# An edge-gated graph layer on one core: from step 10 on the loads of h are issued by ScalarE's queue, GpSimd issues only gathers, and group 1's rows are made in other steps

## The chip, the cores and the metric

One core of a Trainium2 chip. The time is device microseconds of one execution; the median over the runs is told. The engines are TensorE (PE; PEld its weight loads), VectorE (DVE), ScalarE (ACT), GpSimd (POOL) and SyncE (SP). Transfers between the memories are issued by SP, ACT or POOL and carried by 16 transfer engines that all issuers share.

## The reference

B = 16 batches, N = 1024 nodes, D = 256 features, one dense adjacency `A` of 1024×1024 whose entries are mostly zero (a random symmetric pattern of density near 0.8% and the diagonal).

```python
pre_u  = einsum('bud,dk->buk', h, W1[:d])
pre_v  = einsum('bvd,dk->bvk', h, W1[d:])
hidden = relu(pre_u[:, :, None] + pre_v[:, None] + b1)
S      = sigmoid(einsum('buvk,ko->buvo', hidden, W2)[..., 0] + b2)
a      = einsum('buv,bud->bvd', S * A, h)
m      = einsum('uv,bud->bvd', A, h) * h
z      = beta1*h + beta2*(a @ Wa + ba) + beta3*(m @ Wm + bm)
```

The kernel evaluates `hidden` and `S` only where `A` is not zero.

## The kernel before

**Tiles and steps.** The 16 batches form four groups g of four. The 1024 nodes v form eight row blocks vt of 128. A block (g, vt) is worked in T = 10 steps, two windows of 64 nodes times five slots of 128 edges. The 32 blocks make 320 steps n; their order is group 0's vt 0 to 5, group 1's vt 0 to 5, then vt 6 and 7 of both, then groups 2 and 3 whole. For each group a table in device memory holds, per node u, the row of products h·W1[:d] (4×256 numbers) and the row of h (as many).

**One step.** `fetch(n)` is a gather issued by GpSimd: 128 rows of the table, 1 MB, into one of eight buffers `fetched`. `expand` (TensorE, tile `pc`) lays the receiving nodes' products beside the edges. `add` (VectorE) adds both; four VectorE operations make the scores; ScalarE takes the sigmoid (`gt`) and scales the edges' one-hot columns (`left`); `aggregate` (TensorE, tile `acc`) sums the edges into nodes. Buffers come free there, and `refill()` then issues the gather eight steps ahead. Another small gather, `fetch_val` (tile `val`), brings the edges' weights. After every second step ScalarE copies `acc` out (`ev`); at a window's end the sums are turned over (tile `LT`), and `block_end` multiplies them with `w_a` and `w_m` and stores the rows.

**The neighbour lists.** `lists(vt)` makes the edges of a row block: it loads 128 columns of the adjacency (`key`, 512 KB), picks the entries with VectorE, marks the edges' nodes (`mark`, rounded to bytes as `few`), and copies each mark to both halves of `whose` by four transfers of 40 KB. Lists 0 to 3 are made in the prologue, 4 to 7 are begun at steps 7, 14, 44 and 82.

**The tables.** `rows(k)` makes 128 rows of a table in two pieces. A piece is eight products of h with `w_u` on TensorE, a copy by ScalarE (tile `tab`) and a store by SyncE (L442); h itself goes from x into the table by `copy_h` on SyncE (L408). Group 0's rows are all made in the prologue, their stores (`table<-fetched`, L444) on SyncE. For the other groups `plan` names the two steps in which the pieces of a block are made, and `made_rows(n)` loads h for them (`load_hT`, L403, tiles `hT` and `wide`, 512 KB) as soon as a buffer is free and the first piece is at most 14 steps away (`AHEAD`). `again` names blocks whose h is loaded a second time for the block's own products.

**Order.** Each engine works its own instructions in the order in which the code issues them; a scheduler sets the semaphores between engines. The prologue is a written script: each letter of `script` issues a row piece (r), a block's products (h), the first eight gathers (f), one stage of a list (a digit), and so on. `after(step, f)` defers f to that step, `do(step)` calls it. SP and ACT together go round eight completion semaphores for their transfers, GpSimd round eight others; an issue waits until the transfer eight places earlier on its round has landed. In the orders below a row is an instruction's line, its kind, what it writes and reads, and the shape; `x4` counts like rows that follow one another.

Of the kernel before, what the change touches and what calls it, by code (L numbers as in the profile page):

```python
# [11 lines left out]
ALU = mybir.AluOpType  # L12
AX = mybir.AxisListType
P = 128
# [3 lines left out]
def kernel(  # L18
# [42 lines left out]
    nc = tc.nc  # L61
    B, N, D = x.shape
    NT = N // P
    DC = D // P
# [3 lines left out]
    W = 64  # L68
    NW = P // W
# [19 lines left out]
    def load_rows(src, n, name, engine=nc.scalar, at_=None):  # L89
        t = const.tile([P, n], FP, name=name) if at_ is None else at_  # L90
        engine.dma_start(t, bass.AP(tensor=src.tensor, offset=src.offset, ap=[[0, P], [1, n]]))
        return t

    def load_weights(src, name, engine=nc.scalar):
        t = const.tile([P, DC, D], FP, name=name)
        engine.dma_start(t, src.rearrange("(c p) k -> p c k", p=P))
        return t
# [3 lines left out]
    def fixed(shape, name, dt=FP):  # L101
        return const.tile(shape, dt, name=name)
# [74 lines left out]
    def spread(parts, v):  # L177
        nc.vector.tensor_copy(parts, v)
        nc.vector.tensor_tensor(parts[W:], v[W:], parts[W:].bitcast(FP), ALU.subtract)
        nc.vector.tensor_scalar(parts, parts.bitcast(FP), edge, None, ALU.mult)  # L180

    b1_p = fixed([P, D], "b1_p", FR)
    bias_p = fixed([P, D], "bias_p", FR)
# [5 lines left out]
    whose = const.tile([P, NT * NW, E], mybir.dt.uint8, name="whose")  # L189
# [31 lines left out]
    EARLY = 4  # L221
# [13 lines left out]

    def lists(vt):
        key = fetched[vt + 1][:, :N] if vt < EARLY else lst.tile([P, N], FP, name="key", bufs=1)
        (nc.sync if vt < EARLY else nc.gpsimd).dma_start(key, adjT[vt * P:(vt + 1) * P, :])
        yield "load"
        R = Rs[vt % EARLY]  # L240
        top = R[:, 4:]
# [64 lines left out]
        nc.scalar.activation(mark, mark, AF.Sign, bias=span[:, 0:1], scale=-1.0)  # L306
        nc.scalar.activation(mark, mark, AF.Relu)
        yield "step"
        if vt < EARLY:
            nc.scalar.copy(few, mark)  # L310
        else:
            nc.gpsimd.tensor_copy(few, mark)
        for w in range(NW):
            for h in range(2):
                nc.gpsimd.dma_start(whose[h * W:(h + 1) * W, vt * NW + w, :], few[w * W:(w + 1) * W])
        pe = aside(vt)
        for j in range(TW):
            nc.tensor.matmul(pe[:, j * NW * RC:(j + 1) * NW * RC], mark[:, j * P:(j + 1) * P],
# [54 lines left out]
    def after(step, f):  # L373
        due.setdefault(step, []).append(f)
# [8 lines left out]
    hTs = {}  # L383
# [16 lines left out]
    def load_hT(k, engine=nc.sync):  # L400
        g, nt = k
        hTs[k] = hT_free.pop(0)
        engine.dma_start(hTs[k].rearrange("p b c n -> p (b c) n"),  # L403
                         xT_rows[:, g * GB * DC:(g + 1) * GB * DC, nt * P:(nt + 1) * P])
# [95 lines left out]
    T = TW * NW  # L500
# [40 lines left out]
    for i in range(COPIES):  # L541
        copy_h(turn[i], nc.sync)

    script = ("r r 0 0", "r r 1 0 0", "r r 1", "r 0 0", "r r 1", "0 2 r 1", "0 0 r r", "1 2 r 1", "v r r 2", "r 1 3",
              "h 2 1 1", "h 2 2 3", "f 2 2 2 w h h h", "m 3 w 3 3 3")
    begun_rows = {}
    marks, pcs, accs, evs, hbs, LTs, lefts = {}, {}, {}, {}, {}, {}, {}

# [4 lines left out]
    def warm(times):  # L553
        acc = psa.tile([P, 2, D], FP, name="acc")
        for i in range(times):
            nc.tensor.matmul(acc, unit, b1_p.unsqueeze(1).to_broadcast([P, 2, D]), start=True, stop=True)

    m = 0
    piece = None
    parts = halves(0)  # L560
    for t, turns_ in enumerate(script):
        step = t - 100
        do(step)
        for c in turns_.split():
            if c == "r":
                k = turn[m % NT]
                if m < NT:
                    begun_rows[k] = rows(k, tabs[m])
                    next(begun_rows[k])
                go(begun_rows[k], step)  # L570
                if m > NT and m - NT + COPIES <= NT:
                    copy_h(turn[m - NT + COPIES - 1], nc.sync)
                m += 1
            elif c == "h":
                go(parts, step)
            elif c == "v":
                fetch_val(3)
                spread(b1_p, b1_b)
                next(parts)
            elif c == "f":  # L580
                for n in range(NF):
                    fetch(n)
                    if n > 2:
                        fetch_val(1)
                    if n in (3, 6):
                        load_hT(turn[NT + n // 6], nc.gpsimd)
                next(made[EARLY])
                w_a = load_weights(Wa, "w_a", nc.gpsimd)
                w_m = load_weights(Wm, "w_m", nc.gpsimd)
            elif c == "m":  # L590
                load_mark(0)
            elif c == "w":
                warm(6)
            else:
                next(made[int(c)], None)
    do(len(script) - 100)

    def scale_late():
        nc.vector.tensor_scalar(ba_b, ba_b, be2, None, ALU.mult)
        nc.vector.scalar_tensor_tensor(bias, bias, be3, ba_b, ALU.mult, ALU.add)  # L600
        spread(bias_p, bias)
        nc.vector.tensor_scalar(ba_c, ba_c, be2, None, ALU.mult)
        nc.vector.scalar_tensor_tensor(bias_c, bias_c, be3, ba_c, ALU.mult, ALU.add)
        nc.scalar.activation(w_a, w_a, AF.Copy, scale=be2)
        nc.scalar.activation(w_m, w_m, AF.Copy, scale=be3)
        hT_free.append(spare_)

# [190 lines left out]
    def plan(blocks, ns):  # L800

        for k, pieces in zip(blocks, ns):
            pending.append((pieces[0], k))
            at.update((n, k) for n in pieces)

    plan(turn[NT:], ((2, 4), (8, 9), (10, 15), (19, 20), (25, 29), (30, 35), (39, 40), (45, 47)))
    for g, first in ((2, 60), (3, 140)):
        plan([(g, vt) for vt in range(NT)], ((first + 9 + 10 * i, first + 14 + 10 * i) for i in range(NT)))
    pending.extend((order.index(k) * T - T + 1, k) for k in again)
# [2 lines left out]

    def made_rows(n):
        nonlocal piece, last
        while pending and (pending[0][1] in hTs or hT_free and pending[0][0] - AHEAD <= n):
            k = pending.pop(0)[1]
            if k not in hTs:
                load_hT(k, nc.gpsimd if n < T else nc.sync)
        if n in at:
            if at[n] != last:  # L820
                last = at[n]
                copy_h(last, nc.sync)
                piece = rows(last)
                next(piece)
            go(piece, n)
# [58 lines left out]
    for n in range(total - 3):  # L884
        k, s = divmod(n, T)
        if n < ROOM:
            gather_to(n - 1)
        pair_ends()
        if n % TW == (n < ROOM) and n // TW + 1 < total // TW:
            load_mark(n // TW + 1)  # L890
        expand(n + 2)
        if n >= ROOM:
            fill(n, False)
        products(n, k, s)
        if n >= ROOM and n % 2 == 0:
            gather_to(n)
        add(n + 1)
        gate(n)
        while behind:
            nc.scalar.copy(*behind.pop(0))  # L900
        do(n)
        if n == 1:
            bias = load_rows(bm, D, "bias", nc.sync, spare[:, 1])
            ba_b = load_rows(ba, D, "ba_b", nc.sync, spare[:, 2])
            bias_c, ba_c = fixed([P, DC], "bias_c"), fixed([P, DC], "ba_c")
            nc.sync.dma_start(bias_c, bm.rearrange("(c p) -> p c", p=P))
            nc.sync.dma_start(ba_c, ba.rearrange("(c p) -> p c", p=P))
            be1 = load_rows(beta1, 1, "be1", nc.sync)
            be2 = load_rows(beta2, 1, "be2", nc.sync)
            be3 = load_rows(beta3, 1, "be3", nc.sync)  # L910
            after(10, scale_late)
        if n == total - 6:
            hbs[BS - 1] = next(t for t in hT_free if t in flat).rearrange("p b c n -> p b (c n)")
            for v, m, f in tails:
                for h, o in tail_rows(x, v, m, f):
                    nc.sync.dma_start(h, o)
        for i in advance.get(n, ()):
            next(made[i], None)
        if n in start_list:
            running.append([made[start_list[n]], True, n])  # L920
            piece_of(running[-1], n)
        if n < ROOM:
            fill(n, False)
        if n == LISTS:
            assert not running and all(next(x, None) is None for x in made)
            lists_done()
            more = main.enter_context(tc.tile_pool(name="more", bufs=1))
            flat.extend(hT_places(more, MORE, NH))
            hT_free.extend(flat[-MORE:])
            minus.append(more.tile([P, P], FR, name="minus"))  # L930
            nc.vector.tensor_scalar(minus[0], ident, -1.0, None, ALU.mult)
        if n == 120:
            nc.vector.tensor_tensor(rest, rest, taken, ALU.subtract)
            nc.gpsimd.partition_all_reduce(longest, rest, P, bass_isa.ReduceOp.max)
            after(n + 12, count_rest)
# [152 lines left out]
```

## Time and profile before

| quantity | value |
|---|---|
| median of 3 runs | 1040.96 us (1038.32 to 1042.02) |
| profiled execution | 1031.14 us |
| its span | 1029.3 us |
| busy: PE, DVE, ACT, POOL | 958.9, 950.4, 886.5, 467.5 us |
| share of 16 transfer engines: GpSimd's gathers, SP's queue, ACT's queue | 76.1%, 20.3%, 0.2% |
| moved | 375.00 MB, 364 GB/s |
| addition of step 0, 7, 8, 12, 20, 50 starts | 58.49, 79.67, 90.00, 111.43, 138.84, 247.88 us |

The profile is of one execution, and its time is 1% below the median of the runs, so terms from the trace are set against its own time. The share of a queue is the time of its packets, as a share of the 16 engines' span. A later block of ten steps takes some 27.5 us. From the additions in the table one reads that the first twelve steps took 52.9 us, about 4.4 each, where later ones take 2.75.

### The profile page before, as it was taken

How to read it: one execution, taken by the hardware profiler on the slowest of the kernel's cores; microseconds unless marked ns; L12 is line 12 of the kernel's file. 1: busy time of each engine (PE TensorE's matmuls, PEld its weight loads, DVE VectorE, ACT ScalarE, POOL GpSimd, SP SyncE). 2: the span in 40 equal slices, each digit the busy share in tenths (PEclk: the TensorE clock that was granted, in tenths of full speed). 3: DMA queues.
4: the chain of work that ended last, by engine and by line, in shares of the span. 5: the costliest groups of instructions: out<-in, count | busy, mean ns of one | idle time of the engine just before them, and what ended most of it. 6: DMA issues, size and time to landing. Idle time of an engine off the chain costs nothing.

```text
span 1029.3 us, 21645 instructions
## 1 busy us (share of the span) xinstructions
PE 958.9 (93%) x6408; PEld 700.3 (68%) x6408; DVE 950.4 (92%) x3302; ACT 886.5 (86%) x2750; POOL 467.5 (45%) x487
## 2 busy tenths in 40 slices
PE   7886789999899999999999999999999999999996
PEld 5754566676567766767677777777777766777663
DVE  7585979988999999998999999999999999999994
ACT  3665777888888989989899999999999999999984
POOL 3367676746246433564333334333343344444430
PEclk9988899999999999999999999999999999999998
DMA  9898998999999999999999999999999999999992
GB/s 326 304 371 305 350 327 287 332 382 343 360 330 334 378 412 392 381 355 391 411 412 408 414 403 413 401 404 408 391 418 390 379 370 364 381 362 378 373 360 73
DMA packets 123199, 375.00 MB, mean 364 GB/s; under 512 B 17616, under 2 KB 76496, under 8 KB 86864
## 3 DMA queue, kind: packets, MB, share of 16 engines
q0 software_dynamic: 50976, 302.73, 76.1%
q1 hardware_dynamic: 71472, 70.27, 20.3%
q8 instruction: 53, 0.87, 0.3%
q10 hardware_dynamic: 624, 0.52, 0.2%
q14 instruction: 74, 0.61, 0.1%
HBM read 377.53 MB, written 50.33 MB: 416 GB/s over the span
## 4 chain that ended last, share of the span: by engine, by line
PE 45%; DVE 28%; issue 12%; ACT 7%; DMA 5%; POOL 2%; another core or an unknown queue 1%; POOLq 0%; DVEq 0%; SPq 0%; ACTq 0%
DVE fetched L653 15%; PE misc L414 13%; DVE fetched L646 11%; PE misc L740 9%; PE pc L616 8%; PE acc L669 8%; PE misc L691 4%; DMA fetched<-table,uidx 3%; ACT left L660 2%; POOL fetched L516 2%; DVE LT L708 1%; PE misc L724 1%; DMA val<-in_adjT_dram,vidx 1%; DMA wide<-in_xT_dram 1%; DVE low L477 1%
## 5 line engine op out<-in xcount | busy, mean ns | idle before, releaser
L516 POOL DMA_INDIRECT fetched<-table,uidx x320 | 342.7, 1071 | 464.6 <-PE acc L669 318.9
L653 DVE SCALAR_TENSOR_TENSOR fetched<-fetched,w_b 128x256 f32<-128x256 f32 x1280 | 476.7, 425 | 0.0
L646 DVE TENSOR_TENSOR fetched<-fetched,pc 128x1024 f32<-128x1024 f32 x320 | 389.8, 1218 | 43.0 <-DMA fetched<-table,uidx 13.8
L660 ACT ACTIVATE left<-left,gt 128x16 f32<-128x16 f32 x1280 | 285.7, 298 | 0.0
L616 PE MATMUL pc<-X,mark 128*128 128x512 f32 x640 | 227.5, 450 | 21.6 <-DVE fetched L646 17.3
L669 PE MATMUL acc<-fetched,left 128*32 128x256 f32 x2560 | 189.9, 388 | 13.0 <-ACT gt L656 4.5
L616 PEld LDWEIGHTS pc<-X,mark 128*128 128x128 f32 x640 | 105.9, 190 | 108.9 <-issue 55.0
L669 PEld LDWEIGHTS acc<-fetched,left 128*32 128x32 f32 x2560 | 74.4, 109 | 92.9 <-issue 30.0
L656 ACT ACTIVATE gt<-sc,b_b 128x4 f32<-128x4 f32 x320 | 96.7, 302 | 39.4 <-DVE fetched L653 31.6
L740 PE MATMUL misc<-w_a,LT 128*128 128x256 f32 x496 | 117.6, 380 | 1.6 <-issue 1.0
L740 PE MATMUL misc<-w_m,LT 128*128 128x256 f32 x496 | 117.3, 380 | 0.0
L653 DVE DVE_READ_ACCUMULATOR fetched<-fetched,w_b 128x1 f32 x1280 | 108.7, 85 | 0.0
L740 PEld LDWEIGHTS misc<-w_a,LT 128*128 128x128 f32 x496 | 93.8, 190 | 16.6 <-issue 1.4
L677 ACT COPY ev<-acc 128x512 f32<-128x512 f32 x160 | 92.2, 577 | 9.8 <-PE misc L414 5.2
L414 PE MATMUL misc<-w_u,wide 128*128 128x256 f32 x384 | 93.4, 392 | 7.2 <-DMA w_u<-in_W_dram 7.1
L624 ACT ACTIVATE left<-onehot,val 128x32 f32<-128x32 bf16 x320 | 99.9, 312 | 0.0
L356 POOL DMA_INDIRECT val<-in_adjT_dram,vidx x80 | 84.9, 1062 | 26.2 <-issue 21.0
L740 PEld LDWEIGHTS misc<-w_m,LT 128*128 128x128 f32 x496 | 89.7, 191 | 9.7
L691 PE MATMUL misc<-ident,ev 128*128 128x128 f32 x642 | 82.8, 274 | 7.1 <-ACT ev L677 3.0
L414 PE MATMUL misc<-w_v,wide 128*128 128x256 f32 x368 | 88.4, 384 | 0.0
L414 PEld LDWEIGHTS misc<-w_u,wide 128*128 128x128 f32 x384 | 74.7, 197 | 19.8 <-DMA w_u<-in_W_dram 7.1
L691 PEld LDWEIGHTS misc<-ident,ev 128*128 128x128 f32 x642 | 74.0, 141 | 17.1 <-ACT ev L677 4.1
(167 smaller groups left out, 1007.6 us busy)
## 6 DMA issues: line engine op xcount, KB each, us to landing
table<-in_x_dram SPq DMA_DIRECT2D x32, 512.0 KB
out_dram<-z SPq DMA_DIRECT2D x62, 256.0 KB
table<-tab SPq DMA_DIRECT2D x48, 256.0 KB
wide<-in_xT_dram SPq DMA_DIRECT2D x16, 512.0 KB
fetched<-table,uidx POOLq DMA_INDIRECT x320
wide<-in_xT_dram SPq DMA_DIRECT2D x4, 1024.0 KB
table<-fetched SPq DMA_DIRECT2D x8, 512.0 KB
hT<-in_xT_dram SPq DMA_DIRECT2D x8, 512.0 KB
```

The costliest lines, as they stand in the source:

```text
L414: nc.tensor.matmul(p[:, bb * D:(bb + 1) * D], hT[:, 2 * h + bb, i, :], wt[:, i, :], start=(i == 0 and not begun), stop=(i == DC - 1), skip ...
L516: nc.gpsimd.indirect_dma_start(out=fetched[at_slot[n]], out_offset=None, in_=table[g], in_offset=bass.IndirectOffsetOnAxis(ap=uidx[:, vt * ...
L616: nc.tensor.matmul(pcs[n][:, c], marks[n // TW][:, j * P:(j + 1) * P], cuts[k][w][:, c], start=True, stop=True)
L624: nc.scalar.activation(lefts[n][:, 1::GB, :], onehot[:, vt * NW + w, j, :].unsqueeze(1).to_broadcast([P, GB // 2, V]), AF.Copy, scale=val[ ...
L646: nc.vector.tensor_tensor(t, t, pcs.pop(n), ALU.add)
L653: nc.vector.scalar_tensor_tensor(t[:, b, :], t[:, b, :], 0.0, w2_b, ALU.max, ALU.mult, accum_out=sc[:, b:b + 1])
L656: nc.scalar.activation(gt, sc, AF.Sigmoid, bias=b2_b)
L660: nc.scalar.activation(lefts[n][:, 2 * b, :], lefts[n][:, 1 + b // 2 * GB, :], AF.Copy, scale=gt[:, b:b + 1])
L669: nc.tensor.matmul(accs[i][b * 2 * V:(b + 1) * 2 * V, r, :], left[:, 2 * b - b % 2:2 * b - b % 2 + 2].rearrange("p k v -> p (k v)"), f[:, ...
L677: nc.scalar.copy(evs[i], accs.pop(i))
L691: nc.tensor.matmul(pt[:, :, FROM[j]:FROM[j] + V], evs[i][:, r, c * P:(c + 1) * P], ident, is_transpose=True, start=(j == of[0]), stop=True ...
L740: nc.tensor.matmul(pz[:, bb * D:(bb + 1) * D], LT[:, 2 * h + bb, i if bb else 1 - i, c, :], wt[:, c, :], start=(i == 1 and bb == 0 and c = ...
```

## The change

Four parts. (A) GpSimd issues nothing but gathers: the `key` loads of lists 4 to 7, the loads of `w_a` and `w_m`, and all 32 transfers of marks into `whose` go from SyncE; lists 4 to 7 have `few` copied by ScalarE, as 0 to 3 have already. (B) In the prologue the loads of h for group 1's first two blocks move: (1,6) to a new letter k of the script, (1,7) to step 0, both on SyncE; `w_a`, `w_m` and the key of list 4 are loaded at step 0. The bias rows' loads are written in the prologue, and their scaling on VectorE (`scale_bias`, which also frees a buffer for h) is its last letter, s; the scaling of `w_a` and `w_m` stays at step 10. (C) Group 1's row pieces are made in other steps. (D) `made_rows` looks 6 steps ahead before step 10 and 14 after, and loads on SyncE before step 10 and on ScalarE's queue from then on.

```diff
 def lists(vt):
-    (nc.sync if vt < EARLY else nc.gpsimd).dma_start(key, ...)
+    nc.sync.dma_start(key, ...)
...
-    if vt < EARLY:
-        nc.scalar.copy(few, mark)
-    else:
-        nc.gpsimd.tensor_copy(few, mark)
+    nc.scalar.copy(few, mark)
...
-            nc.gpsimd.dma_start(whose[...], few[w * W:(w + 1) * W])
+            nc.sync.dma_start(whose[...], few[w * W:(w + 1) * W])
...
-    ..., "f 2 2 2 w h h h", "m 3 w 3 3 3")
+    ..., "f 2 2 2 k w h h h", "m 3 w 3 3 3 s")
...
+def scale_bias():           # the five VectorE lines of scale_late (seven operations)
+    ...
+    hT_free.append(spare_)
...
         fetch(n)
-        if n in (3, 6):
-            load_hT(turn[NT + n // 6], nc.gpsimd)
-    next(made[EARLY])
-    w_a = load_weights(Wa, "w_a", nc.gpsimd)
-    w_m = load_weights(Wm, "w_m", nc.gpsimd)
+    bias = load_rows(bm, D, "bias", nc.sync, spare[:, 1])
+    ...                      # ba_b, bias_c, ba_c, be1, be2, be3 as before
+elif c == "k":
+    load_hT(turn[NT])
+elif c == "s":
+    scale_bias()
...
-plan(turn[NT:], ((2, 4), (8, 9), (10, 15), (19, 20), (25, 29), (30, 35), (39, 40), (45, 47)))
+plan(turn[NT:], ((4, 6), (9, 11), (13, 18), (19, 21), (23, 28), (29, 31), (33, 38), (39, 41)))
...
-while pending and (... pending[0][0] - AHEAD <= n):
+while pending and (... pending[0][0] - (AHEAD if n >= T else 6) <= n):
-        load_hT(k, nc.gpsimd if n < T else nc.sync)
+        load_hT(k, nc.scalar if n >= T else nc.sync)
...
-if n == 1:
-    bias = load_rows(...)    # and the other seven
-    after(10, scale_late)
+if n == 0:
+    for i in advance[0]:
+        next(made[i], None)
+    load_hT(turn[NT + 1])
+    next(made[EARLY])
+    w_a, w_m = load_weights(Wa, "w_a", nc.sync), load_weights(Wm, "w_m", nc.sync)
+    after(10, scale_weights)
```

Three places show how instructions move. The first is GpSimd from the gather of step 7 (into `fetched_189`, the eighth buffer) to that of step 8 (into `fetched_182`, the first); `table_60` is group 0's table and `uidx` holds the edges' nodes. Before:

```order
L516 DMA fetched_189<-table_60,uidx 128x2048
L356 DMA val<-in_adjT_dram,vidx 128x1
L238 DMA key<-in_adjT_dram 128x1024
L96 DMA w_a<-in_Wa_dram 128x2x256
L96 DMA w_m<-in_Wm_dram 128x2x256
L315 DMA whose<-few 64x640 x4
L403 DMA wide<-in_xT_dram 128x8x128
L315 DMA whose<-few 64x640 x4
L516 DMA fetched_182<-table_60,uidx 128x2048
```

Now, one gather of weights is left between them, so twelve transfers have gone from there:

```order
L513 DMA fetched_188<-table_60,uidx 128x2048
L353 DMA val<-in_adjT_dram,vidx 128x1
L513 DMA fetched_189<-table_60,uidx 128x2048
L353 DMA val<-in_adjT_dram,vidx 128x1
L513 DMA fetched_182<-table_60,uidx 128x2048
```

The second is SyncE at the end of group 0's table, before:

```order
L444 DMA table_60<-fetched_182 128x1024
L444 DMA table_60<-fetched_183 128x1024
L408 DMA table_60<-in_x_dram 128x4x256
L444 DMA table_60<-fetched_184 128x1024
L444 DMA table_60<-fetched_185 128x1024
L444 DMA table_60<-fetched_186 128x1024
L444 DMA table_60<-fetched_187 128x1024
L91 DMA hT_204<-in_bm_dram 128x256
```

And now, where the four copies of list 1's marks stand ahead of the last store (those of list 0 stand earlier, behind the first store of this kind):

```order
L441 DMA table_60<-fetched_182 128x1024
L441 DMA table_60<-fetched_183 128x1024
L405 DMA table_60<-in_x_dram 128x4x256
L441 DMA table_60<-fetched_184 128x1024
L441 DMA table_60<-fetched_185 128x1024
L441 DMA table_60<-fetched_186 128x1024
L312 DMA whose<-few 64x640 x4
L441 DMA table_60<-fetched_187 128x1024
L91 DMA hT_204<-in_bm_dram 128x256
```

The third is ScalarE in the later blocks, in the changed kernel; `gt` and `left` belong to the gates of two steps, `X` is prepared for the next block, and the load of h (L400) stands between the copy of a `mark` and the next gate:

```order
L666 ACTIVATE left<-left,gt 128x16 x4
L683 COPY ev_6482<-acc 128x512
L548 CAST mark<-whose 128x640
L400 DMA hT_204<-in_xT_dram 128x8x128
L662 ACTIVATE gt<-sc,b_b 128x4
L630 ACTIVATE left<-onehot,val 128x2x16
L666 ACTIVATE left<-left,gt 128x16 x4
```

Before, that load stood on SyncE between two stores of a table, and ScalarE had no transfer there. In all SyncE goes from 24 loads of h by `made_rows` to none from step 10 on, and ScalarE from none to 25.

More of the change, by code (lines that the diff above doesn't have):

```diff
@@ L237, in lists @@
         key = fetched[vt + 1][:, :N] if vt < EARLY else lst.tile([P, N], FP, name="key", bufs=1)
-        (nc.sync if vt < EARLY else nc.gpsimd).dma_start(key, adjT[vt * P:(vt + 1) * P, :])
+        nc.sync.dma_start(key, adjT[vt * P:(vt + 1) * P, :])
         yield "load"
@@ L308, in lists @@
         yield "step"
-        if vt < EARLY:
-            nc.scalar.copy(few, mark)
-        else:
-            nc.gpsimd.tensor_copy(few, mark)
+        nc.scalar.copy(few, mark)
         for w in range(NW):
             for h in range(2):
-                nc.gpsimd.dma_start(whose[h * W:(h + 1) * W, vt * NW + w, :], few[w * W:(w + 1) * W])
+                nc.sync.dma_start(whose[h * W:(h + 1) * W, vt * NW + w, :], few[w * W:(w + 1) * W])
         pe = aside(vt)
@@ L544 @@
     script = ("r r 0 0", "r r 1 0 0", "r r 1", "r 0 0", "r r 1", "0 2 r 1", "0 0 r r", "1 2 r 1", "v r r 2", "r 1 3",
-              "h 2 1 1", "h 2 2 3", "f 2 2 2 w h h h", "m 3 w 3 3 3")
+              "h 2 1 1", "h 2 2 3", "f 2 2 2 k w h h h", "m 3 w 3 3 3 s")
     begun_rows = {}
@@ L556, in warm @@
             nc.tensor.matmul(acc, unit, b1_p.unsqueeze(1).to_broadcast([P, 2, D]), start=True, stop=True)
+    def scale_bias():
+        nc.vector.tensor_scalar(ba_b, ba_b, be2, None, ALU.mult)
+        nc.vector.scalar_tensor_tensor(bias, bias, be3, ba_b, ALU.mult, ALU.add)
+        spread(bias_p, bias)
+        nc.vector.tensor_scalar(ba_c, ba_c, be2, None, ALU.mult)
+        nc.vector.scalar_tensor_tensor(bias_c, bias_c, be3, ba_c, ALU.mult, ALU.add)
+        hT_free.append(spare_)
     m = 0
@@ L584 @@
                         fetch_val(1)
-                    if n in (3, 6):
-                        load_hT(turn[NT + n // 6], nc.gpsimd)
-                next(made[EARLY])
-                w_a = load_weights(Wa, "w_a", nc.gpsimd)
-                w_m = load_weights(Wm, "w_m", nc.gpsimd)
+                bias = load_rows(bm, D, "bias", nc.sync, spare[:, 1])
+                ba_b = load_rows(ba, D, "ba_b", nc.sync, spare[:, 2])
+                bias_c, ba_c = fixed([P, DC], "bias_c"), fixed([P, DC], "ba_c")
+                nc.sync.dma_start(bias_c, bm.rearrange("(c p) -> p c", p=P))
+                nc.sync.dma_start(ba_c, ba.rearrange("(c p) -> p c", p=P))
+                be1 = load_rows(beta1, 1, "be1", nc.sync)
+                be2 = load_rows(beta2, 1, "be2", nc.sync)
+                be3 = load_rows(beta3, 1, "be3", nc.sync)
+            elif c == "k":
+                load_hT(turn[NT])
+            elif c == "s":
+                scale_bias()
             elif c == "m":
@@ L596, with scale_weights @@
     do(len(script) - 100)
[L598 to L603, printed above, removed]
+    def scale_weights():
         nc.scalar.activation(w_a, w_a, AF.Copy, scale=be2)
         nc.scalar.activation(w_m, w_m, AF.Copy, scale=be3)
-        hT_free.append(spare_)
     def expand(n):
@@ L814, in made_rows @@
         nonlocal piece, last
-        while pending and (pending[0][1] in hTs or hT_free and pending[0][0] - AHEAD <= n):
+        while pending and (pending[0][1] in hTs or hT_free and pending[0][0] - (AHEAD if n >= T else 6) <= n):
             k = pending.pop(0)[1]
             if k not in hTs:
-                load_hT(k, nc.gpsimd if n < T else nc.sync)
+                load_hT(k, nc.scalar if n >= T else nc.sync)
         if n in at:
@@ L901 @@
         do(n)
-        if n == 1:
[L903 to L910, printed above, removed]
-            after(10, scale_late)
+        if n == 0:
[5 more added lines that the diff above has]
+            after(10, scale_weights)
         if n == total - 6:
@@ L916 @@
                     nc.sync.dma_start(h, o)
-        for i in advance.get(n, ()):
+        for i in advance.get(n, ()) if n else ():
             next(made[i], None)
```

## The prediction

> **What bounds the kernel now.** I read the head of the page first, then the row by engine of the chain that ended last.
>
> ```profile
> span 1029.3 us, 21645 instructions
> PE 958.9 (93%) x6408; PEld 700.3 (68%) x6408; DVE 950.4 (92%) x3302; ACT 886.5 (86%) x2750; POOL 467.5 (45%) x487
> PE 45%; DVE 28%; issue 12%; ACT 7%; DMA 5%; POOL 2%; another core or an unknown queue 1%; POOLq 0%; DVEq 0%; SPq 0%; ACTq 0%
> ```
>
> TensorE and VectorE share the end; ScalarE is close behind; GpSimd, which the change relieves most, is busy 45%. Shares over the whole span hide the stages, so next comes the table of busy time by stretch. Its columns are the window, its length, busy us of PE, PEld, DVE, ACT and POOL, granted clock, DMA share and GB/s.
>
> ```profile
> 58.00:82.20 24.20, 19.04 (x103) 12.33 (x104) 22.21 (x73) 17.20 (x54) 14.41 (x18) 0.93 1.02 387
> 82.20:90.00 7.80, 2.74 (x22) 1.29 (x19) 0.08 (x3) 4.09 (x11) 6.28 (x9) 0.85 0.76 247
> 90.00:97.00 7.00, 5.73 (x26) 4.30 (x27) 6.42 (x21) 2.43 (x8) 5.47 (x6) 0.68 0.97 348
> 97.00:111.40 14.40, 8.50 (x42) 5.73 (x40) 8.89 (x32) 4.00 (x15) 10.43 (x11) 0.89 0.94 327
> 111.40:139.00 27.60, 26.49 (x168) 18.61 (x165) 25.07 (x97) 24.17 (x73) 19.61 (x20) 0.94 0.97 339
> 560.00:720.00 160.00, 160.00 (x1120) 120.68 (x1119) 159.22 (x535) 153.92 (x480) 60.30 (x58) 1.00 1.03 407
> 720.00:1000.00 280.00, 272.82 (x1903) 198.24 (x1902) 279.33 (x966) 265.81 (x872) 113.61 (x105) 1.00 0.99 380
> ```
>
> Three regimes: up to 82 us the transfer engines are full; from 82 to 111 VectorE works 15.4 us of 29.2 and TensorE 17.0; from 111 on TensorE or VectorE is nearly full, and from 560 to 720 both. So little can be won after 139 us; the early hole is the place. What stands in it is GpSimd's stream between the gather of step 7 and that of step 8, and the addition that waits for it (start, us, instruction, idle before and what ended it).
>
> ```profile
> 68.52 1.09 POOL L516 DMA_INDIRECT fetched<-table,uidx  x1 [0.30 <-issue]
> 70.36 0.99 POOL L356 DMA_INDIRECT val<-in_adjT_dram,vidx  x1 [0.75 <-DMA fetched<-table,uidx]
> 71.35 0.60 POOL L238 DMA_DIRECT2D key<-in_adjT_dram  x1
> 72.97 0.73 POOL L96 DMA_DIRECT2D w_a<-in_Wa_dram  x1 [1.02 <-DMA fetched<-table,uidx]
> 73.69 0.72 POOL L96 DMA_DIRECT2D w_m<-in_Wm_dram  x1
> 75.77 1.08 POOL L315 DMA_DIRECT2D whose<-few  x2 [1.35 <-ACT X L427]
> 77.35 0.52 POOL L315 DMA_DIRECT2D whose<-few  x1 [0.51 <-DMA wide<-in_xT_dram]
> 79.87 0.52 POOL L315 DMA_DIRECT2D whose<-few  x1 [2.00 <-DMA val<-in_adjT_dram,vidx]
> 80.42 0.93 POOL L403 DMA_DIRECT2D wide<-in_xT_dram  x1
> 81.91 2.07 POOL L315 DMA_DIRECT2D whose<-few  x4 [0.56 <-ACT left L660]
> 84.29 1.06 POOL L516 DMA_INDIRECT fetched<-table,uidx  x1 [0.30 <-PE misc L691]
> 90.00 1.22 DVE L646 TENSOR_TENSOR fetched<-fetched,pc 128x1024 f32<-128x1024 f32 x1 [7.72 <-DMA fetched<-table,uidx]
> ```
>
> The gather of step 8 goes out at 84.29, 12.9 us after the last small gather ended (71.35): ahead of it stood twelve plain transfers and the lane waits in front of them. VectorE then waits 7.72 us for it. The window row gives the DMA share there as 0.76.
>
> **The change, part by part.**
>
> *GpSimd relieved at the start.* Between those gathers one small gather is left. The issue of step 8's gather is then no longer held by POOL's order, but by TensorE's aggregate of step 0, which frees its buffer, and by the completion lane. The gain is at most the wait, 7.72. At least it is the unused part of the transfer engines in that window, (1−0.76)×7.80 = 1.9 us, since the 1 MB gather must still be moved by engines that are full (1.02) before 82.2. Nearer is the upper middle: the plain transfers that are taken out from ahead (512 KB of columns, 512 KB of h, the small ones) are not gone, but go behind. I take **−5**. VectorE works 0.08 of the 7.80 us of that window, so no other work of its own covers the wait.
>
> *The marks' copies on SyncE.* The eight 40 KB copies of lists 0 and 1 now stand ahead of the last store of group 0's table. SyncE must wait there for ScalarE as GpSimd did:
>
> ```profile
> 41.51 2.14 POOL L315 DMA_DIRECT2D whose<-few  x4 [7.03 <-ACT L L322]
> 35.44 5.50 SPq L444 DMA_DIRECT2D table<-fetched  x4
> 50.41 1.06 POOL L516 DMA_INDIRECT fetched<-table,uidx  x1 [6.75 <-DMA be<-in_beta_dram]
> 66.33 0.72 ACT L310 CAST few<-made 128x640 uint8<-128x640 f32 x1
> ```
>
> The last store ended issuing at 40.94 and would now follow 41.51+2.14 = 43.65: 2.7 us later, and with it, at worst, the first gather (50.41). At best nothing, because a later short transfer is what the row names. I take half, **+1**. The copies of list 3 wait for ScalarE's copy that starts at 66.33; behind them on SyncE stand the load of h for block (1,7), the key of list 4 and w_a, w_m, of which the row piece of step 9 needs the first. The steps between hide that wait; if it grew beyond them, the piece of step 9 would be late.
>
> *The scaling of the bias* (seven VectorE operations) moves from step 10 to the prologue:
>
> ```profile
> 106.15 0.35 DVE L599 TENSOR_SCALAR hT<-hT,be 128x256 f32<-128x256 f32 x1
> 108.48 0.22 DVE L603 SCALAR_TENSOR_TENSOR bias_c<-bias_c,be,ba_c 128x2 f32<-128x2 f32 x1
> ```
>
> They run from 106.15 to 108.70, 2.55 us. Ahead of the first addition they would cost that if VectorE were the last to be ready; but the steps up to 8 start as their gathers land, 2.4 to 2.7 us apart, and VectorE catches up. Taken out at 106 they give nothing certain, since ScalarE's wait beside them ends later (109.28). **0**, bounds −2.5 to +2.5.
>
> *The other plan for the rows of group 1.* Sixteen pieces stay sixteen. One that lay at step 2, in a stretch with TensorE 19.04 of 24.20 us busy, now lies where TensorE is nearly full; a piece is 8 matrix products and a copy:
>
> ```profile
> L414 PE MATMUL misc<-w_u,hT x128: 377/379/754, 67.8 to 648.4; 128*128 128x256 f32 x128
> 109.28 0.58 ACT L427 COPY tab<-misc 128x512 f32<-128x512 f32 x1 [6.60 <-remote]
> 102.69 6.57 another core or an unknown queue
> ```
>
> The first row's columns are the shortest, median and longest ns of one; products overlap, so eight take at least part of 8×0.38 = 3.0. For one piece shifted I take **+1**, bounds 0 to 3.0. The other two rows are the early hole's second half: ScalarE waits 6.60 us for something that the profile doesn't name, just at the copy of a row piece of step 9, and the chain goes through it. The changed plan has other pieces there (9 and 11, not 8, 9 and 10), and fewer transfers are issued late by POOL. Whether that wait goes isn't shown; bounds 0 to −6.6, half taken, **−3**.
>
> *25 loads of h on ScalarE's queue, and four copies of marks on ScalarE.* Before, 24 went from SyncE (columns as above) and one from GpSimd; ScalarE's queue issued six stores at the end:
>
> ```profile
> L403 SPq DMA_DIRECT2D hT<-in_xT_dram x8: 183/558/8521, 110.3 to 586.6; - x8
> L403 SPq DMA_DIRECT2D wide<-in_xT_dram x16: 379/475/5874, 113.6 to 699.2; - x16
> L790 ACTq DMA_DIRECT2D out_dram<-hT x6: 373/490/963, 1016.3 to 1022.3; - x6
> L312 POOL CAST few<-made x4: 724/914/918, 146.9 to 410.0; 128x640 uint8<-128x640 f32 x4
> ```
>
> 25×0.49 = 12.3 us at the median of ScalarE's own issues, and 4×0.73 = 2.9 us of copies, together 15 of the 143 us in which ScalarE is idle. Most of it is covered while VectorE or TensorE is the last to be ready; if that cover is gone, all 15 count. The lower end is 0, the upper the blocked case below. I take **+2**. GpSimd saves four copies of 0.91; its gathers wait for TensorE's aggregates, so nothing. SyncE gets its stores out earlier; no engine waits for them within two blocks: 0.
>
> The Trainium skill bears on this, "DMA: Bandwidth & Descriptors", section "Issuing engines are not separate DMA queues": transfers from all issuing engines run on the same 16 engines and interleave, and several issuers save only the time to start a transfer. By that rule the load on another queue moves no byte faster, and the early gain is only what the order on GpSimd cost; with the idle share alone (−1.9 in place of −5) the sum would be 3 us higher. The window row with 0.76 between stretches of 1.02 and 0.97 agrees that some time is there beyond bytes, and how much, no row says.
>
> Sum: −5 +1 +0 +1 −3 +2 = −4. The profiled execution took 1031.14 us (span 1029.3, 1.8 around it); the median of the three runs, 1040.96, is 9.8 us above. −4 on either gives 1027 and **1037**; the forecast is on the median.
>
> **The rivals.**
>
> *ScalarE is blocked as SyncE was (slower).* SyncE's issues of the same loads swelled where the transfer engines are full:
>
> ```profile
> 586.64 8.52 SPq L403 DMA_DIRECT2D hT<-in_xT_dram  x1
> 619.16 1.38 SPq L403 DMA_DIRECT2D wide<-in_xT_dram  x1
> 647.13 2.71 SPq L403 DMA_DIRECT2D wide<-in_xT_dram  x1
> 672.64 2.53 SPq L403 DMA_DIRECT2D wide<-in_xT_dram  x1
> 699.20 5.87 SPq L403 DMA_DIRECT2D wide<-in_xT_dram  x1
> ```
>
> These five take 21.0 us. On ScalarE they would stand ahead of the gates of the next step, and ScalarE has 160.00−153.92 = 6.1 us free there: about +15, with the early −4 that is 1041+11 = 1052. It decides once the five exceed 6.1+4 us, a mean of 2.0 each. For it: the swelling is in this very stage. Against it: right ahead of each stand SyncE's stores of the tables, whose pieces may fill that queue, while ScalarE's holds nothing else. Chance 0.14. The Trainium skill, "Perfetto Trace Analysis", section "DMA Instruction — HWDGE (DVE, Sync)", says that the block which generates descriptors is shared between sequencers and locked for exclusive use, and that the wait for the lock is in the shown duration; by that, a long store of SyncE would hold ScalarE's load too. The trace of before has no load on ScalarE's queue beside a long store, so it can't show it.
>
> *A late give-back (same).* A third source of transfers no longer waits behind SyncE's stores and so takes turns from the gathers, where both TensorE and VectorE are full (560 to 720) and the DMA share is 1.03. A load of 512 KB at the 407 GB/s of that row fills the engines for 1.3 us; where three of them in that stretch come ahead of a gather that would have come first, +4 cancels the gain: 1041. Chance 0.15.
>
> *The early wait stays (same).* If the engines' full share means that bytes, not POOL's order, delay the gather of step 8, −1.9 meets +1, +1 and the unnamed wait stays: 1041. Chance 0.12.
>
> *The prologue starts late (slower).* The last table store 2.7 us later and the scaling's 2.55 ahead of the first addition add, 5.3 in all; with the early gain at 1.9 only, that is +3.4, and 1044. It decides where the first gather starts later than 50.41 by more than the early gain. Chance 0.11.
>
> **How the numbers follow.** 0.3% is 3.1 us, about what a measurement of this kernel can tell from no change. The forecast, faster, has 0.48, its own range 1027 to 1037.8: it includes that both halves of the early hole close (−7.7, −6.6 without the costs is 1027). Same 0.15+0.12 = 0.27; slower 0.14+0.11 = 0.25. From 1027 to 1048 lie the forecast, both cases of no change and the late start; about 0.1 is left on each side, for the blocked queue above and a larger early gain below.
>
> **What would show it.** Right: the gather of step 8 is issued near 72 instead of 84.29 and the addition's wait of 7.72 falls under 3; the first gather at 50 to 52; the window 97 to 111 with VectorE above 10 us busy; loads of h on ScalarE's queue at 0.4 to 0.6 each; 560 to 720 with the same work. Wrong: loads of h of 2 us or more on ScalarE's queue with VectorE waiting behind the gates; the first gather past 53; additions in 560 to 720 waiting for their gathers; the unnamed waits of ScalarE turning up again at another place.

## The result and the profile after

The changed kernel is faster: 1031.16 us median against 1039.0, fifteen runs each on one chip, ratio 0.9928, 95% interval 0.9908 to 0.9947. That is −7.5 us (−5.5 to −9.6); the forecast was −4.

The profiled execution took 1031.57 us, in the middle of its fifteen runs. That of before, 1031.14, was below all fifteen of its own (1034.51 to 1045.88). So the ends of the two traces can't be subtracted; they are read for their stages. First the same rows of the page after as before.

```profile
span 1029.8 us, 21597 instructions
PE 959.6 (93%) x6408; PEld 698.6 (68%) x6408; DVE 948.8 (92%) x3302; ACT 890.7 (86%) x2754; POOL 439.4 (43%) x441
PE 52%; DVE 23%; DMA 9%; issue 7%; ACT 6%; another core or an unknown queue 1%; POOL 1%; SPq 0%; DVEq 0%; ACTq 0%; POOLq 0%
```

GpSimd has 28 us less work, ScalarE 4 us more. The same windows after:

```profile
58.00:82.20 24.20, 17.47 (x89) 11.23 (x88) 23.02 (x75) 15.24 (x46) 16.44 (x16) 0.86 1.04 387
82.20:90.00 7.80, 4.40 (x32) 2.76 (x24) 4.41 (x18) 3.61 (x10) 4.98 (x6) 0.97 1.05 389
90.00:97.00 7.00, 4.49 (x25) 2.39 (x26) 3.20 (x8) 4.80 (x16) 3.80 (x4) 0.55 1.02 393
97.00:111.40 14.40, 14.27 (x91) 10.79 (x91) 14.40 (x54) 13.15 (x42) 9.72 (x10) 1.00 1.06 390
560.00:720.00 160.00, 160.00 (x1121) 120.48 (x1119) 159.16 (x536) 153.86 (x483) 59.77 (x57) 1.00 1.03 408
```

From 82 to 111 VectorE works 22.0 us, not 15.4, and the transfer share is 1.02 to 1.06 where it was 0.76 to 0.97. The stage from 560 to 720 is unchanged. Addition 12 comes at 103.92 (before 111.43), addition 20 at 128.58 (138.84), addition 60 at 274.21 (279.48); from addition 150 on the two traces run together (549.79 and 549.76). As the execution of before was quicker than all its fifteen runs, this pair can't tell whether the lead of 10.3 us at step 20 was lost by then; the first two experiments can.

GpSimd's stream between the gathers of steps 7 and 8, and VectorE behind it:

```profile
68.01 0.99 POOL L513 DMA_INDIRECT fetched<-table,uidx  x1 [2.06 <-DMA fetched<-table,uidx]
69.31 1.00 POOL L353 DMA_INDIRECT val<-in_adjT_dram,vidx  x1 [0.30 <-issue]
71.02 0.99 POOL L513 DMA_INDIRECT fetched<-table,uidx  x1 [0.71 <-DVE eq L326]
84.70 1.22 DVE L652 TENSOR_TENSOR fetched<-fetched,pc 128x1024 f32<-128x1024 f32 x1 [0.69 <-PE pc L622]
93.80 0.69 DVE L245 SCALAR_TENSOR_TENSOR key<-key,ukey 128x512 f32<-128x512 f32 x1 [6.50 <-DMA key<-in_adjT_dram]
72.16 21.61 DMA key<-in_adjT_dram
```

The gather of step 8 goes out at 71.02, not 84.29, and its wait of 7.72 is gone. A new one stands one step later: VectorE waits 6.50 us for the key of list 4. The last row is of the chain: the key's load is issued at 72.16, behind the marks that wait for ScalarE on SyncE's queue, and takes 21.61 us to land.

### The profile page after: what moved, and what is told of

Read it like the earlier page. It is cut to its first block, busy times and chain, and to the rows that moved or that the text cites. A ratio compares the mean times of both kernels' runs of the same rounds, so it can differ in the third digit from the quotient of the medians.

```text
span 1029.8 us, 21597 instructions
## 1 busy us (share of the span) xinstructions
PE 959.6 (93%) x6408; PEld 698.6 (68%) x6408; DVE 948.8 (92%) x3302; ACT 890.7 (86%) x2754; POOL 439.4 (43%) x441
## 4 chain that ended last, share of the span: by engine, by line
PE 52%; DVE 23%; DMA 9%; issue 7%; ACT 6%; another core or an unknown queue 1%; POOL 1%; SPq 0%; DVEq 0%; ACTq 0%; POOLq 0%
PE misc L411 14%; PE misc L746 11%; DVE fetched L659 11%; PE pc L622 10%; PE acc L675 9%; DVE fetched L652 8%; PE misc L697 4%; DMA wide<-in_xT_dram 4%; DMA key<-in_adjT_dram 2%; DMA fetched<-table,uidx 2%; ACT left L666 2%; PE misc L730 1%; DVE LT L714 1%; DMA fetched<-in_adjT_dram 1%; PE misc L415 1%
## 5 line engine op out<-in xcount | busy, mean ns | idle before, releaser
L622 PE MATMUL pc<-X,mark 128*128 128x512 f32 x640 | 229.8, 451 | 19.9 <-DVE fetched L652 13.7
L675 PE MATMUL acc<-fetched,left 128*32 128x256 f32 x2560 | 185.5, 389 | 8.8 <-ACT left L630 4.4
L675 PEld LDWEIGHTS acc<-fetched,left 128*32 128x32 f32 x2560 | 72.3, 109 | 87.0 <-issue 26.3
L659 DVE DVE_READ_ACCUMULATOR fetched<-fetched,w_b 128x1 f32 x1280 | 98.4, 77 | 0.0
L411 PE MATMUL misc<-w_v,wide 128*128 128x256 f32 x368 | 91.9, 395 | 3.1 <-DMA wide<-in_xT_dram 3.1
```

What stands on the lines that cost most here:

```text
L411: nc.tensor.matmul(p[:, bb * D:(bb + 1) * D], hT[:, 2 * h + bb, i, :], wt[:, i, :], start=(i == 0 and not begun), stop=(i == DC - 1), skip ...
L622: nc.tensor.matmul(pcs[n][:, c], marks[n // TW][:, j * P:(j + 1) * P], cuts[k][w][:, c], start=True, stop=True)
L659: nc.vector.scalar_tensor_tensor(t[:, b, :], t[:, b, :], 0.0, w2_b, ALU.max, ALU.mult, accum_out=sc[:, b:b + 1])
L675: nc.tensor.matmul(accs[i][b * 2 * V:(b + 1) * 2 * V, r, :], left[:, 2 * b - b % 2:2 * b - b % 2 + 2].rearrange("p k v -> p (k v)"), f[:, ...
```

## The experiments

Twelve kernels in three sets; each set ran on one chip against its own runs of the kernel before. Those had medians of 1019.2 us in the first set, 1021.5 in the second and 1038.6 in the third, so ratios are compared, not microseconds.

**1. The loads of h back on SyncE** (`loads_on_sp`).

```diff
-load_hT(k, nc.scalar if n >= T else nc.sync)
+load_hT(k, nc.sync)
```

> The changed kernel with the loads of h from step 10 on given back to SyncE; everything else as changed. Theory 1 (the gain is made in the first 24 steps, ScalarE's queue does little): ratio to before 0.993 or a little less, SyncE's loads and table stores of 560 to 720 us swell again to 2 to 19 us, but nobody waits for them. Rival 2 (the early gain of 10 us is eaten by step 150, where the profiled executions of both kernels meet, and the measured 7.5 us come from SyncE's queue, which no longer mixes loads with stores): ratio 0.999 to 1.001.

Ratio 0.9921 (0.9895 to 0.9946): the whole gain is there without ScalarE's queue.

**2. The same loads on ScalarE, alone** (`loads_on_act`), the kernel before with `nc.sync` replaced by `nc.scalar` in that line from step 10 on.

> The kernel before with one edit: the loads of h from step 10 on go from ScalarE's queue. Theory 1: ratio 1.000 to 1.002, the wait of 7.7 us before step 8 and the unnamed wait of 6.6 us stay. Rival 2: ratio 0.992 to 0.994 with an unchanged start. Both expect ScalarE's loads at 0.37 us each and SyncE's table stores below 10 us in 560 to 720.

Ratio 1.0033 (1.0006 to 1.0060), +3.4 us: a small loss, a little above theory 1 and opposite to rival 2. The wait before step 8 stays, at 7.76 us. This kernel and that of experiment 1 ran on one chip, and the lead of the latter is kept: its addition 20 comes 6.8 us earlier, addition 60 7.4, addition 150 11.4 and addition 300 7.4 (127.56, 261.85, 527.87, 942.26 against 134.36, 269.23, 539.27, 949.62). Against the kernel of experiment 3, on the same chip too, it is 5.5, 7.3, 7.5 and 11.6. So time won early was not given back by step 150 there.

On SyncE's queue the picture changes as both theories had said. The first two rows are of the kernel before and of this one, the third of the changed kernel with loads on SyncE; then ScalarE's loads here and SyncE's loads in experiment 1 (shortest, median, longest ns):

```profile
L442 SPq DMA_DIRECT2D table<-tab x48: 319/490/19006, 70.4 to 761.2; - x48
L442 SPq DMA_DIRECT2D table<-tab x48: 319/339/577, 72.2 to 752.4; - x48
L439 SPq DMA_DIRECT2D table<-tab x48: 319/582/15732, 86.2 to 745.1; - x48
L403 ACTq DMA_DIRECT2D wide<-in_xT_dram x16: 374/374/375, 126.4 to 697.8; - x16
L400 SPq DMA_DIRECT2D wide<-in_xT_dram x18: 379/434/10022, 71.2 to 678.8; - x18
```

With the loads off SyncE's queue a table store never takes more than 0.58 us to issue here; with them it took up to 19.0 in the kernel before. Yet the kernel with the long issues is not the slower one. It is not that nobody ever waits for these stores: in experiment 1 the first gather of group 2 (step 160) waited 10.39 us for one, and its addition 5.21 us for that gather:

```profile
553.04 0.99 POOL L513 DMA_INDIRECT fetched<-table,uidx  x1 [10.39 <-DMA table<-tab]
560.70 1.22 DVE L652 TENSOR_TENSOR fetched<-fetched,pc 128x1024 f32<-128x1024 f32 x1 [5.21 <-DMA fetched<-table,uidx]
```

Neither the trace of before nor that after has such a wait.

**3. The new plan alone** (`plan_alone`), the kernel before with the changed tuple of steps.

> The kernel before with one edit: the new steps for group 1's row pieces. Theory 1 with the unnamed wait due to the pieces of steps 8, 9 and 10: the wait of 6.6 us before ScalarE's copy of a row piece is gone, ratio 0.994 to 0.997. Rival (the wait belongs to the crowded start, wherever the pieces lie): it stays or turns up elsewhere before step 24, ratio 0.999 to 1.002.

Ratio 1.0008 (0.9981 to 1.0036): no change that the interval shows, as the rival said. The wait at step 8 is even longer here:

```profile
92.16 1.22 DVE L646 TENSOR_TENSOR fetched<-fetched,pc 128x1024 f32<-128x1024 f32 x1 [9.11 <-DMA fetched<-table,uidx]
```

The unnamed wait is absent, but so it is in every trace of the first two sets, also in those with the old plan. The plan is not what took it away.

**4. GpSimd relieved, alone** (`gathers_alone`), the kernel before with only:

```diff
-(nc.sync if vt < EARLY else nc.gpsimd).dma_start(key, ...)
+nc.sync.dma_start(key, ...)
-nc.gpsimd.tensor_copy(few, mark)       # lists 4 to 7
+nc.scalar.copy(few, mark)
-nc.gpsimd.dma_start(whose[...], few[...])
+nc.sync.dma_start(whose[...], few[...])
...                                     # key of list 4, w_a, w_m: SyncE, at step 0
```

> The kernel before with one part of the change: keys, marks' copies, w_a and w_m go from SyncE and the marks are rounded on ScalarE; h's first loads stay on GpSimd, the plan, the bias's scaling and SyncE's later loads of h stay. Theory 1 (the order on GpSimd carries the gain): ratio 0.993 to 0.996, the gather of step 8 issued before 77 us. Rival (it takes the plan or the early scaling too): 0.998 to 1.001 with the wait of 7.7 us turned into others before step 13.

Ratio 0.9932 (0.9906 to 0.9959), −6.9 us (−9.6 to −4.2): this part alone has a gain as large as the whole change, even with the early loads of h still on GpSimd. The gather of step 8 goes out at 77.00 (expected: before 77) and its addition, at 88.46, waits 1.66 us:

```profile
77.00 1.04 POOL L513 DMA_INDIRECT fetched<-table,uidx  x1 [1.39 <-DVE fetched L647]
88.46 1.22 DVE L640 TENSOR_TENSOR fetched<-fetched,pc 128x1024 f32<-128x1024 f32 x1 [1.66 <-DMA fetched<-table,uidx]
```

**5. The changed kernel again** (`after_again`).

> The changed kernel as it stands, for a comparison on the same chip as the three beside it. Theory 1 (the early steps carry the gain): ratio to before 0.991 to 0.995, VectorE's wait for the key of list 4 at 5 to 7 us again. If the ratio is nearer to 0.996 here, the size of the gain differs between chips, and the variants are to be judged against this row.

Ratio 0.9943 (0.9922 to 0.9963), −5.8 us: the size holds within its interval in another set, where the kernel before took 1021.5 us. The wait for the key was 1.6 us here, not the 5 to 7 expected, so the 6.50 of the first trace is not a fixed cost. One of ScalarE's 25 loads was not short in this trace:

```profile
114.26 3.55 ACTq L400 DMA_DIRECT2D wide<-in_xT_dram  x1
```

The next gate (`gt`) started at 117.85, 0.04 us after that issue ended.

**6. The bias scaled late again** (`bias_late`): the letter s taken out, `after(10, scale_bias)` put back.

> The changed kernel with the seven VectorE operations of the bias's scaling back at step 10 (the spare buffer of h comes free there, too). By the prediction's 0 for this part: same ratio as the changed kernel beside it, within 0.2%. Rival (VectorE is busy from step 11 on, so 2.55 us count there): the changed kernel's ratio plus 0.002 to 0.003.

Ratio 0.9944 (0.9922 to 0.9966), beside 0.9943: nothing speaks against the prediction's 0, but intervals of 0.002 to either side can't rule out the rival's 0.002 to 0.003.

**7 and 8. The new wait taken away.** In `key_first` the key of list 4, in `both_first` also h of block (1,7), is written ahead of list 3's marks:

```diff
+load_hT(turn[NT + 1])                  # both_first only
+next(made[EARLY])
 for i in advance[0]:
     next(made[i], None)
-load_hT(turn[NT + 1])                  # both_first only
-next(made[EARLY])
```

> The changed kernel with the load of list 4's key written ahead of list 3's marks on SyncE, so that it no longer waits for ScalarE at 69 us. Theory 1 (time won early is kept at least in part): VectorE's wait of 6.5 us before step 9 falls under 2, ratio to before 0.988 to 0.991. Rival 2 (won time is given back by step 150): the wait goes and the ratio stays 0.992 to 0.994. A third outcome, the load pushes back the first gathers by its 1.3 us of transfer: 0.993 to 0.995.

> The changed kernel with two loads, h of block (1,7) and the key of list 4, written ahead of list 3's marks on SyncE, so neither waits for ScalarE at 69 us. Theory 1 (an early microsecond is worth about half of one at the end, as 10 became 7.5): both VectorE's wait for the key and TensorE's wait for h before step 10 fall under 1 us, ratio to before 0.986 to 0.991. Rival (1 MB more ahead of the first gathers delays them as much): the first eight additions come 2 us or more later, ratio 0.992 to 0.996.

Ratios 0.9956 (0.9928 to 0.9983) and 0.9962 (0.9938 to 0.9985): no gain over the changed kernel. Both miss theory 1's range; `key_first` lies above the ranges of its two other outcomes as well, though its interval reaches into them. In the first the wait for the key is gone and two others have come, TensorE's for h; in the second VectorE still waits for the key and TensorE for a later block's h:

```profile
93.88 3.62 PE L411 MATMUL misc<-w_u,wide 128*128 128x256 f32 x8 [1.94 <-DMA wide<-in_xT_dram]
110.66 3.57 PE L411 MATMUL misc<-w_u,wide 128*128 128x256 f32 x8 [2.17 <-DMA wide<-in_xT_dram]
```

```profile
91.88 0.69 DVE L245 SCALAR_TENSOR_TENSOR key<-key,ukey 128x512 f32<-128x512 f32 x1 [4.51 <-DMA key<-in_adjT_dram]
112.57 3.42 PE L411 MATMUL misc<-w_u,wide 128*128 128x256 f32 x8 [3.85 <-DMA wide<-in_xT_dram]
```

The first fence is of `key_first`, the second of `both_first`. From 82 to 111 us the share of the transfer engines is 1.05 in both traces; the order of the loads changed who waited, and not the time. The ratio of `both_first` is just above its rival's range, but not for the rival's reason: against `after_again`, on the same chip, none of its first eight additions came more than 0.4 us later, and that of step 7 came 1.9 us earlier (82.25 and 84.12).

**9. Only the place on GpSimd's queue** (`marks_later`), the kernel before with the copies of the marks of lists 2 and 3 still on GpSimd, sent at steps 8 and 10:

```diff
+if vt in (2, 3):
+    after(8 + 2 * (vt - 2), send)
+else:
+    send()
```

> The kernel before with nothing moved off GpSimd; only the eight copies of the marks of lists 2 and 3 are issued there at steps 8 and 10 instead of between the gathers of steps 7 and 8. If the place on the queue is what counts: the gather of step 8 is issued before 79 us in place of 84, the wait before its addition falls to 2 to 5 us, ratio 0.995 to 0.998. If it is GpSimd as issuer that counts: the wait is spread over the gathers that follow, ratio 0.999 to 1.001.

```profile
77.36 1.55 POOL L521 DMA_INDIRECT fetched<-table,uidx  x1 [0.30 <-issue]
87.61 1.22 DVE L651 TENSOR_TENSOR fetched<-fetched,pc 128x1024 f32<-128x1024 f32 x1 [4.37 <-issue]
```

The gather goes out 6.9 us earlier than in the first trace of before, and addition 8 comes at 87.61 instead of 90.00, as the first theory said. The ratio, 0.9988 (0.9965 to 1.0011), lies between the two forecasts, and its interval reaches into both. It does say that this move is worth 3.6 us at most, less than the least that experiment 4 allows (4.2). Against that trace the lead is 2.5 us at step 20 and none at step 50 (247.90 and 247.88); where it went isn't shown.

**10 to 12. Fewer bytes early.** The first three copies of x into group 1's table are put off, in the changed kernel (`copies_later`), in the kernel before (`copies_later_before`) and in the relieved one (`gathers_copies`):

```diff
-copy_h(last, nc.sync)
+if n < 19:
+    after(24 + n // 5, lambda k=last: copy_h(k, nc.sync))
+else:
+    copy_h(last, nc.sync)
```

> The changed kernel with the first three copies of x into group 1's table (512 KB read and 512 KB written each, steps 4, 9 and 13) put off to steps 24 to 26. Theory 3 (after the change the stretch from 58 to 139 us is bound by the bytes that the transfer engines move, share 1.04): step 20 comes 3 to 6 us earlier than in the changed kernel, and the ratio to before falls by 0.001 to 0.005 below the changed kernel's 0.994. Rival (the order on the queues still sets the steps): step 20 within 1.5 us, ratio 0.993 to 0.996.

> The kernel before with the same copies put off (there from steps 2, 8 and 10). Theory 3: before the change the hole at step 8 is not one of bytes (share 0.76), so the wait of 7.7 us stays at 5 to 9 us, and the ratio is 0.998 to 1.001. Rival (bytes bind here as well): the wait falls by 3 us or more, 0.994 to 0.997.

> The kernel before with GpSimd relieved of keys, marks and weights, and the three copies put off to steps 24 to 26. Theory 3: 0.002 to 0.005 below the relief alone (0.993), that is 0.988 to 0.991. Rival: 0.992 to 0.995.

Ratios 0.9922 (0.9888 to 0.9956), 0.9993 (0.9966 to 1.0019) and 0.9911 (0.9879 to 0.9942). Before the change, 3 MB of early traffic put off (read and written) give nothing that the interval shows, and the wait at step 8 stays:

```profile
88.48 1.22 DVE L646 TENSOR_TENSOR fetched<-fetched,pc 128x1024 f32<-128x1024 f32 x1 [7.00 <-DMA fetched<-table,uidx]
```

So these bytes were not what held that gather. After the change both ratios are low, but the intervals reach into the ranges of theory 3 and of its rival, and experiment 1 is as low without this edit (0.9921). Addition 20 of `copies_later` came at 126.86 against 128.58 in the first trace after, 1.7 us earlier where theory 3 wanted 3 to 6; that of `gathers_copies` came at 135.07, later than the 128.51 of `gathers_alone` on another chip. That bytes bind the early steps after the change is suggested by the share of 1.02 to 1.06 and not shown.

## Why the prediction was right, and where its size was off

*Where the time came from* was right: the early steps, through GpSimd's queue; the gather of step 8 at 71.02 (forecast near 72), the late stage unchanged. Experiment 4 gives that part alone −6.9 us.

*The term for GpSimd was probably too small, and one reason for it was wrong.* I took −5 for one wait of 7.72 and +1 for the marks' copies on SyncE, −4 together; the kernel of experiment 4, which holds both, gave −6.9 (−9.6 to −4.2). For the relief further on I took nothing, since "its gathers wait for TensorE's aggregates". GpSimd's waits from 82 to 139 us, before and then after, say otherwise:

```profile
POOL val L356 <- issue: 6.4, 21, 0.3
POOL fetched L516 <- PE acc L669: 3.4, 3, 1.8
POOL fetched L516 <- issue: 3.4, 11, 0.3
```

```profile
POOL fetched L513 <- PE acc L675: 5.1, 3, 2.6
POOL val L353 <- issue: 4.9, 16, 0.3
POOL fetched L513 <- PE pc L622: 3.1, 3, 1.1
```

The columns are the total, the times and the longest wait. Before, in these 57 us,

```profile
82.00:139.00 57.00, 43.66 (x253) 30.07 (x252) 40.67 (x149) 34.89 (x107) 42.00 (x44) 0.88 0.93 325
L356 POOL DMA_INDIRECT val<-in_adjT_dram,vidx x22 | 23.1, 1050 | 6.7 <-issue 6.4 <-DVE fetched L653 0.3
L516 POOL DMA_INDIRECT fetched<-table,uidx x16 | 16.3, 1018 | 8.3 <-PE acc L669 3.4 <-issue 3.4 <-PE pc L616 1.2
```

GpSimd was busy 42.0 us, and 9.8 more passed as the 0.3 us ahead of most gathers that nothing accounts for: 51.8 of 57, with 3.4 of waiting for aggregates. From the gather of step 8, at 84.29, to 110 us it went from one issue to the next without any other pause. So in that stretch GpSimd's queue was full, though GpSimd is busy 45% over the whole span, and a plain transfer on it put off all gathers behind it. That would explain why moving eight of them by two or three steps (experiment 9) did little, and taking them off gave the gain. It is not shown further than step 8: of VectorE's waits from 82 to 139 us the trace puts 8.3 on gathers, 7.72 of them at step 8, and 5.4 on something that it doesn't name. How the 6.9 us divide over the single transfers was not tried.

*The −3 for the unnamed wait had no ground.* Such waits add up to 16.8 us in the trace of before and to 19.3 in that after, at other places, which was one of the prediction's own signs of being wrong:

```profile
ACT tab L424 <- remote: 9.4, 2, 5.2
POOL fetched L513 <- remote: 6.9, 5, 1.6
DVE fetched L652 <- remote: 2.3, 2, 1.6
```

They are absent from all traces of the first two sets, whose runs of before were 2% quicker, and present in the third. They go with the chip or the hour at which it ran, not with the change; what they are stays open. Without this term the sum is −1, against −7.5 measured. That the forecast came near is in that part luck: a term wrong in kind stood in for one that was too small.

*The small terms* agree with what was measured, within wide intervals. The first gather went out at 51.73, 1.3 us later (taken: +1). The plan: +0.8 (−1.9 to 3.7; taken: +1). The bias: 0, though on a misreading: the steps up to 8 do not "start as their gathers land, 2.4 to 2.7 us apart". In the trace of before only one of the additions 1 to 7 shows a wait for its gather (1.29, at step 1), they are 2.5 to 4.6 us apart, and VectorE was busy 22.21 of those 24.20 us. ScalarE's queue: +3.4 (0.6 to 6.1; taken: +2) in the kernel before; in the changed kernel the price may be smaller, as −8.1 us without it stand beside −7.5 and −5.8 with it, in three different sets. The parts tried alone, −6.9, +0.8, 0 and +3.4, add up to −2.7 and not to −7.5; with intervals of 2 to 3 us to either side that is no contradiction, but it isn't shown that they simply add.

The price of ScalarE's queue is not a matter of swollen issues:

```profile
L400 ACTq DMA_DIRECT2D wide<-in_xT_dram x16: 374/374/375, 117.2 to 708.3; - x16
L400 ACTq DMA_DIRECT2D hT<-in_xT_dram x9: 374/374/767, 100.5 to 596.5; - x9
L439 SPq DMA_DIRECT2D table<-tab x48: 319/339/9572, 81.1 to 761.9; - x48
```

Twenty-five loads at 0.37 are 9.4 us of ScalarE's time, so the 3.4 would be about a third of that; that this is where it comes from is argued, not shown. The first rival, ScalarE blocked for 2 us and more from 560 to 720, did not come: none of these loads took more than 0.38 us there. The single issue of 3.55 us in experiment 5 lies at 114 us. SyncE's swelling is not carried over with the loads. The long stores that are left in this trace lie before 100 us, where SyncE still carries other loads; from there on none took more than 0.59.

By the Trainium skill, "Perfetto Trace Analysis", section "DMA Instruction — HWDGE (DVE, Sync)", the block that generates descriptors is shared and locked for exclusive use; as the prediction read it, a long store of SyncE would hold ScalarE's load. The trace of `both_first` shows a case where it did not: two of ScalarE's loads went out in 1.09 us together, inside a store of SyncE that took 5.51:

```profile
95.97 5.51 SPq L439 DMA_DIRECT2D table<-tab  x1
99.75 1.09 ACTq L400 DMA_DIRECT2D hT<-in_xT_dram  x2
```

And beside the issue of 3.55 us in experiment 5 SyncE was issuing nothing. Neither fits that reading of the page; what makes an issue long stays open.

*The new wait for the key* was named only as a place that was covered ("the steps between hide that wait"): in the first trace it wasn't, and 6.50 us stood at step 9 in place of 7.72 at step 8. Experiments 7 and 8 show no gain from moving it.

## What to carry to other kernels

An engine's share over the whole span can hide a stage in which its queue is full: add to its busy time the small fixed gap ahead of every issue, and look who ended its waits in that stage alone. A wait that a late transfer causes can be worth less than its length, as the wait for the key was, which others replaced; test the move of the one transfer before its length is booked as gain. And ratios between kernels want runs on one chip: the kernel before differed by 2% between sets on different chips here, almost three times the gain in question.

## What the hardware showed

A load of h issued by ScalarE's queue took 0.374 us, shortest and median alike, where the same load from SyncE's queue took up to 10.0 in experiment 1, and taking the loads away in the kernel before brought SyncE's longest table store from 19.0 us to 0.58. The small gathers, 128 numbers each, cost GpSimd as much as the 1 MB ones: 1.05 and 1.02 us, with 0.3 us ahead of most. I had expected neither.
